# Normalizing tiles on GpSimd: mean and power applied directly, or through an offset from VectorE

## The chip, the cores and the metric

The kernel runs on one core of one Trainium2 chip. The core has five engines with a queue each: TensorE (PE; its weight loads are listed apart as PEld), VectorE (DVE), ScalarE (ACT), GpSimd (POOL) and SyncE (SP, which here issues transfers). Each works through its own instructions in order and waits on semaphores for the others. The metric is the device time of one execution in microseconds; lower is better.

## The reference, cut to what matters

A transformer block on x of shape (2, 1024, 256) with a context of (2, 154, 192), in float32, 16 heads of 64:

```python
h = _layernorm(x, ln1_g, ln1_b)
x = _attention(h, h, sa_wq, sa_wk, sa_wv, sa_wo, sa_bo) + x
h = _layernorm(x, ln2_g, ln2_b)
x = _attention(h, cond_emb, ca_wq, ca_wk, ca_wv, ca_wo, ca_bo) + x
h = _layernorm(x, ln3_g, ln3_b)
p = h @ ff_w1 + ff_b1
a, gate = (p[..., :D_FF], p[..., D_FF:])
h = a * jax.nn.gelu(gate, approximate=False) @ ff_w2 + ff_b2
return h + x
...
def _layernorm(x, g, b, eps=1e-05):
    mu = jnp.mean(x, axis=-1, keepdims=True)
    var = jnp.var(x, axis=-1, keepdims=True)
    return (x - mu) * jax.lax.rsqrt(var + eps) * g + b
```

## The kernel before, in words

All of x stays on the chip, in tiles of 128 rows by 256 columns, eight tiles for each of the two batches. The kernel has one long program, written out in order by hand: nothing reorders it. It runs in three parts. First comes self-attention (16 units of one batch and two heads, each in eight steps, loop `for p in range(SA)`), then cross-attention (16 units in three steps, loop `for c in range(CA)`), then the feed-forward (64 steps, loop `for k in range(2 * FU)`). The parts overlap: work for a later part is put on lists (`work`, `side`, `outs`, `later`, `slow`) and taken from them a piece at a time between the steps of the part that is running.

A normalization (`norm_pieces`) is cut into pieces. `stats` takes mean and variance of one tile on DVE (lines 242 and 243) into the tile `mv`. `deviation` works on a pair of tiles: it adds epsilon (line 248) and raises the result to the power −0.5 on POOL (line 252), which gives `rstd`. `normalize`, also on a pair, forms `off` = −mean · rstd on DVE (line 258, 128 x 2 elements) and then, for each of the two tiles, computes x · rstd + off. `turn` transposes the result on PE (line 286, four transposes per pair, the second of which already reads the second tile), and `store` inside it applies gain and shift (lines 297 and 301). `mv`, `var`, `rstd` and `off` come from a pool with four buffers for each name.

Which engine applies x · rstd + off depends on `narrow(kind, b)`. It is true for both batches of the first normalization and for batch 0 of the second; there ACT does it (line 276), or, in the very first normalization, ACT for one tile and POOL for the other. It is false for batch 1 of the second normalization (in the cross-attention loop) and for both batches of the third (batch 0 late in the cross-attention loop, batch 1 in the feed-forward loop); there POOL does both tiles (line 273). That makes 3 normalizations of 4 pairs each, 12 pairs and 24 POOL instructions.

`norm_beside` spreads a normalization over steps: in one step a pair gets its stats, in the next its deviation, then its normalize, then its turn. Within one step the pieces are issued as turn, (stats, put on `slow`), deviation of a later pair, normalize; so on POOL the power of the next pair stands just ahead of the normalize of this one, and on DVE the offset stands ahead of the next pair's stats.

Of the names in the trace: L901 scales the probabilities of cross-attention on POOL, after the reciprocal L898 on DVE; L650 does it in self-attention. L1074 is a matrix product of the feed-forward (`pa`, `pb`, `pc`); L1103, L1105, L1119, L1122 and L1131 are DVE's sums over those products, L1117, L1123 and L1099 are ACT's activations and copies, L1124 and L1133 POOL's products of the two halves. L500 is the output projection of an attention, L953 probabilities by values, L873 the scores of cross-attention.

Of the kernel before, what the change touches and what calls it, by code (L numbers as in the profile page):

```python
# [8 lines left out]
F32 = mybir.dt.float32  # L9
AF = mybir.ActivationFunctionType  # L10
ALU = mybir.AluOpType
AX = mybir.AxisListType

P = 128
# [4 lines left out]
def tile_transformer_block(ctx: ExitStack, tc: tile.TileContext, a: dict, out: bass.AP):  # L19
    nc = tc.nc  # L20
# [41 lines left out]
    small = ctx.enter_context(tc.tile_pool(name="small", bufs=4))  # L62
# [105 lines left out]
    for n in names[2:]:  # L168
        own = rows[row_of[n] - n_cols:row_of[n] - n_cols + n_of[n], :]
# [53 lines left out]
    def norm_pieces(kind, b, first=False):  # L223

        ln = {"sa": "ln1", "ca": "ln2", "ff": "ln3"}[kind]
        g0, b0 = row_of[ln + "_g"], row_of[ln + "_b"]  # L230
        st = {}
        nh = NC if kind == "ff" else NH
        order = tile_order(kind)

        def stats(t):
            if t == 0:
                st["hT"] = hT[kind, b] = p2.tile(
                    [P, nh, NC * S // nh], F32, tag="hT", name=f"hT_{ln}_{b}")
            if t % 2 == 0:
                st["mv", t] = small.tile([P, 2, 2], F32, tag="mv", name=f"mv_{ln}_{b}_{t}")  # L240
            s6 = small.tile([P, 6], F32, tag="st", name=f"st_{ln}_{b}_{t}")
            nc.vector.bn_stats(s6, xt[b, order[t] // GT][:, order[t] % GT, :])
            nc.vector.bn_aggr(st["mv", t // 2 * 2][:, t % 2, :], s6)

        def deviation(t):
            mv = st["mv", t]
            var = small.tile([P, 2], F32, tag="var", name=f"var_{ln}_{b}_{t}")
            (nc.vector if first else nc.gpsimd).tensor_scalar(
                var, mv[:, :, 1], EPS, 1.0, op0=ALU.add, op1=ALU.mult
            )  # L250
            rstd = small.tile([P, 2], F32, tag="rstd", name=f"rstd_{ln}_{b}_{t}")
            nc.gpsimd.tensor_tensor(rstd, var, power, ALU.pow)
            st["rstd", t] = rstd

        def normalize(t):
            rstd = st["rstd", t]
            off = small.tile([P, 2], F32, tag="off", name=f"off_{ln}_{b}_{t}")
            nc.vector.scalar_tensor_tensor(
                off, st["mv", t][:, :, 0], -1.0, rstd, op0=ALU.mult, op1=ALU.mult
            )  # L260
            if narrow(kind, b) and not first:
                xn = st["hT"][:, :, t * P // 2:(t + 2) * P // 2].rearrange(
                    "p c (i d) -> p c i d", i=2)
                st["xn", t] = [xn[:, c].rearrange("p i d -> p (i d)") for c in range(nh)]
            else:
                xn = pp_.tile([P, nh, 2, D // nh], F32, tag="P", name=f"xn_{ln}_{b}_{t}")
                flat = xn.rearrange("p c i d -> p (c i d)")
                st["xn", t] = [flat[:, i * P:(i + 1) * P] for i in range(2 * D // P)]
            for i in range(2):
                xs = xt[b, order[t + i] // GT][:, order[t + i] % GT, :]  # L270
                xs, own = xs.rearrange("p (c d) -> p c d", c=nh), xn[:, :, i, :]
                if not narrow(kind, b) or first and i == 1:
                    nc.gpsimd.tensor_scalar(
                        own, xs, rstd[:, i:i + 1], off[:, i:i + 1], op0=ALU.mult, op1=ALU.add)
                else:
                    nc.scalar.activation(
                        own, xs, AF.Identity, bias=off[:, i:i + 1], scale=rstd[:, i:i + 1])

        def turn(t):

            n = 2 if first else 1
            bank = mm_tile if first and t == 2 else spare["bank"]
            ph = [bank(f"ph_{ln}_{b}_{t}_{i}") for i in range(n)]
            for i in range(2 * D // P):

                nc.tensor.transpose(  # L286
                    ph[i * n * P // (2 * D)][:, i % (2 * D // P // n) * P:][:, :P],
                    st["xn", t][i], ident)

            def store():  # L290
                k = NC * 2 * P // nh
                for c in range(nh):
                    own = st["hT"][:, c, t // 2 * k:(t // 2 + 1) * k]
                    turned = ph[c * n // nh][:, c % (nh // n) * k:][:, :k]
                    gain, shift = cols[:, g0 + c:g0 + c + 1], cols[:, b0 + c:b0 + c + 1]
                    if spare["turned"] or first and c < nh // 2:
                        nc.vector.tensor_scalar(
                            own, turned, gain, shift, op0=ALU.mult, op1=ALU.add
                        )
                    else:  # L300
                        nc.scalar.activation(own, turned, AF.Identity, bias=shift, scale=gain)

            return store

        return (
            [lambda t=t: stats(t) for t in range(NT)],
            *([lambda t=t, f=f: f(t) for t in range(0, NT, 2)] for f in (deviation, normalize, turn)),
        )

    def tile_order(kind):  # L310

        if kind == "ff":
            return list(range(NT))
        return [t for i in range(NT // 2) for t in (i, NT // 2 + i)]

    def narrow(kind, b):

        return kind == "sa" or kind == "ca" and b < B - 1
# [947 lines left out]
    with tc.manual_schedule():  # L1266
# [11 lines left out]
        own = [ps_s.tile([P, 2, HB], F32, tag="s", name=f"first_{r}") for r in range(2)]  # L1278
# [47 lines left out]
        for p in range(SA):  # L1326
# [28 lines left out]
            if hg == LAG:  # L1355
                f = (ui - NPAIR // 2 - 1) * EC
# [184 lines left out]
```

## Time and profile before

| | us |
|---|---|
| median of 3 runs | 1070.75 (1070.31 to 1073.51) |
| the profiled execution | 1067.09 |
| its span in the trace | 1065.1 |

The profile lists, for each engine, the time in which an instruction was running. Rows of groups give line, engine, operation, output <- inputs, shape, count, then total busy time and mean nanoseconds of one, then the idle time of the engine just before and whom it waited for. Rows of the timeline give start, duration, engine, line and operation, with idle time before it in brackets. Ends of PE's matrix products are modelled, so idle time of PE is seen only where a product starts late.

### The profile page before, as it was taken

What the parts mean: (1) busy time and instruction counts of PE and PEld (TensorE: products, weight loads), DVE (VectorE), ACT (ScalarE), POOL (GpSimd) and SP (SyncE); (2) the same over time, 40 slices, a digit from 0 to 9 for tenths busy, and PEclk for the clock granted to TensorE, in tenths of its full rate; (3) what the DMA queues carried; (4) which work ended last, traced back from release to release, by engine and by line L of the source; (5) the groups of instructions that cost most, each with busy time, mean ns of one, the idle gap of its engine ahead of it and who ended that gap; (6) DMA issues with size and microseconds to landing.
All of it is one profiled execution on the core that took longest, in us unless ns stands there. A gap on an engine that the chain in (4) does not pass through costs nothing.

```text
span 1065.1 us, 48669 instructions
## 1 busy us (share of the span) xinstructions
PE 1055.6 (99%) x20228; PEld 707.7 (66%) x20228; DVE 882.5 (83%) x1321; ACT 647.3 (61%) x2096; POOL 778.4 (73%) x1652
## 2 busy tenths in 40 slices
PE   8999999999999999999999999999999999999998
PEld 6556656656555555667655655566866668788998
DVE  5789999998989989999999899979877877654555
ACT  5766767677666666666776676666666554343231
POOL 2677777778777777777777777777767875499984
PEclk9999999999999999999999999999999999999999
DMA  3131122121021121111102101126776545000000
GB/s 102 36 75 54 29 68 54 25 63 41 22 58 28 34 51 34 39 34 34 45 14 54 44 14 38 33 57 161 175 172 165 123 98 125 5 11 11 21 10 30
DMA packets 86046, 60.95 MB, mean 57 GB/s; under 512 B 32123, under 2 KB 74563, under 8 KB 85827
## 3 DMA queue, kind: packets, MB, share of 16 engines
q1 hardware_dynamic: 84450, 57.07, 22.1%
q8 instruction: 159, 2.61, 1.0%
q10 hardware_dynamic: 1376, 0.79, 0.3%
q14 instruction: 61, 0.49, 0.2%
HBM read 27.91 MB, written 2.10 MB: 28 GB/s over the span
## 4 chain that ended last, share of the span: by engine, by line
PE 90%; DVE 3%; POOL 2%; DMA 2%; SPq 1%; issue 1%; ACT 1%; DVEq 0%; POOLq 0%; ACTq 0%
PE po L578 19%; PE s L526 19%; PE py_ca L500 5%; PE py_sa L500 5%; PE pk_sa L369 5%; PE pq_sa L369 5%; PE pq_ca L369 4%; PE pv_sa L405 4%; PE poc L953 4%; PE pb L1074 4%; PE pq L1219 4%; PE sc L873 3%; PE pa L1074 2%; PE pc L1074 2%; PE pf L1249 1%; PE ph_ln L286 1%
## 5 line engine op out<-in xcount | busy, mean ns | idle before, releaser
L650 POOL TENSOR_SCALAR p<-p,rd,ee 128x512 f32<-128x512 f32 x512 | 392.6, 772 | 88.6 <-DVE rd L640 86.6
L537 ACT ACTIVATE p<-s,st 128x512 f32<-128x512 f32 x512 | 345.3, 687 | 174.1 <-DVE st L712 170.6
L712 DVE TENSOR_REDUCE st<-s 128x2 f32<-128x1024 f32 x256 | 308.7, 1207 | 57.7 <-issue 17.5
L675 DVE STREAM_TRANSPOSE pT<-p 128x1024 f32<-128x1024 f32 x256 | 302.5, 1219 | 1.6 <-POOL p L650 1.4
L526 PE MATMUL s<-k_sa,q_sa 64*32 64x512 f32 x4096 | 255.8, 591 | 0.8 <-DVE k_sa L390 0.6
L578 PE MATMUL po<-pT,held_v 64*32 64x256 f32 x8192 | 238.9, 376 | 0.0
L578 PEld LDWEIGHTS po<-pT,held_v 64*32 64x32 f32 x8192 | 178.2, 106 | 69.8 <-issue 26.5
L526 PEld LDWEIGHTS s<-k_sa,q_sa 64*32 64x32 f32 x4096 | 87.4, 106 | 93.1 <-issue 46.8
L890 ACT ACTIVATE p<-sc,neg 128x154 f32<-128x154 f32 x256 | 96.4, 406 | 73.5 <-DVE rden L898 70.6
L901 POOL TENSOR_SCALAR p<-p,rden 128x154 f32<-128x154 f32 x256 | 97.3, 401 | 47.3 <-DVE rden L898 47.0
L537 ACT ACTIVATION_READ_ACCUMULATOR p<-s,st 128x1 f32 x512 | 103.7, 203 | 0.0
L555 POOL TENSOR_TENSOR dd<-st 128x8 f32<-128x8 f32 x128 | 25.8, 202 | 69.0 <-DMA st<-st 65.1
L500 PE MATMUL py_ca<-ca_wo,o_ca 128*128 128x256 f32 x256 | 60.2, 383 | 0.0
L500 PE MATMUL py_sa<-sa_wo,o_sa 128*128 128x256 f32 x256 | 59.5, 386 | 0.0
L500 PEld LDWEIGHTS py_sa<-sa_wo,o_sa 128*128 128x128 f32 x256 | 47.3, 190 | 18.0 <-issue 5.9
L369 PE MATMUL pq_ca<-hT_ln,ca_wq 64*64 64x512 f32 (+1 forms) x576 | 58.5, 589 | 0.3 <-DMA ca_wq<-in_L_xattn_ca_wq_dram 0.3
L879 DVE TENSOR_REDUCE neg<-sc 128x6 f32<-128x924 f32 (+1 forms) x48 | 47.8, 995 | 12.1 <-PE sc L873 12.1
L369 PE MATMUL pq_sa<-hT_ln,sa_wq 64*32 64x512 f32 (+1 forms) x976 | 57.3, 586 | 0.0
L890 ACT ACTIVATION_READ_ACCUMULATOR p<-sc,neg 128x1 f32 x256 | 56.7, 221 | 0.0
L369 PE MATMUL pk_sa<-hT_ln,sa_wk 64*32 64x512 f32 x960 | 56.5, 590 | 0.1
L917 DVE STREAM_TRANSPOSE pT_ca<-p 128x480 f32<-128x480 f32 (+1 forms) x96 | 52.9, 586 | 0.9 <-POOL p L901 0.8
L500 PEld LDWEIGHTS py_ca<-ca_wo,o_ca 128*128 128x128 f32 x256 | 47.4, 190 | 8.2 <-issue 1.9
(158 smaller groups left out, 1479.5 us busy)
## 6 DMA issues: line engine op xcount, KB each, us to landing
wf<-pT_ca SPq DMA_DIRECT2D x128, 128.0 KB, 2.4
st<-st SPq DMA_DIRECT2D x512, 1.0 KB, 1.8
held_v<-held_v SPq DMA_DIRECT2D x32, 256.0 KB, 3.8
sa_wq<-in_L_xattn_sa_wq_dram SPq DMA_DIRECT2D x32, 128.0 KB, 2.9
sa_wk<-in_L_xattn_sa_wk_dram SPq DMA_DIRECT2D x32, 128.0 KB, 3.3
sa_wv<-in_L_xattn_sa_wv_dram SPq DMA_DIRECT2D x16, 256.0 KB, 4.3
ca_wq<-in_L_xattn_ca_wq_dram SPq DMA_DIRECT2D x32, 128.0 KB, 3.7
wf<-in_L_xattn_ff_w_dram SPq DMA_DIRECT2D x12, 256.0 KB, 3.1
```

Of the source, the lines that this page charges most:

```text
L369: nc.tensor.matmul(pq[r][f:f + m, at:at + n], lhsT=wt[own, c, f:f + m], rhs=h[own, c, t0:t0 + n], start=(c == 0), stop=(c == NH - 1), tile ...
L500: nc.tensor.matmul(py[:, e * D:(e + 1) * D], lhsT=o[:, i, (t + e) * P:(t + e + 1) * P], rhs=wo[kind][:, g * HP + i, :], start=(i == 0), st ...
L526: nc.tensor.matmul(sc[a4 * KB:(a4 + 1) * KB, j, :], lhsT=q[r, c:c + KB], rhs=k[r, h * HB:(h + 1) * HB], start=True, stop=True, tile_positi ...
L537: nc.scalar.activation(pr[:, j, :], sc[:, j, :], AF.Exp, bias=st[:, 0, 0, i, j:j + 1], accum_out=st[:, 0, 1, i, j:j + 1],)
L578: nc.tensor.matmul(po[a2][d:d + KB, :QH // 2], lhsT=v[e][r, t, d:d + KB], rhs=pT[r, d // DH * NK + n, :], start=(t == 0 and e == 0), stop= ...
L650: nc.gpsimd.tensor_scalar(pr[:, j, :], pr[:, j, :], own["rd"][:, c:c + 1], own["ee"][:, 0, c:c + 1], op0=ALU.mult, op1=ALU.mult,)
L675: nc.vector.transpose(halves[h][:, :, c:c + KB], slots[p]["p"][i].rearrange("p j (n k) -> p (j n) k", k=KB))
L712: nc.vector.tensor_reduce(st[:, 0, 0, i, :], sc[i], AX.X, ALU.max, negate=True)
L890: nc.scalar.activation(pr_[:, j, i, :T], sc[:, j, i * T:(i + 1) * T], AF.Exp, bias=neg[:, j, i:i + 1], accum_out=den[:, j, i:i + 1],)
L901: nc.gpsimd.tensor_scalar(pr_[:, j, i, :T], pr_[:, j, i, :T], rden[:, j, i:i + 1], 1.0, op0=ALU.mult, op1=ALU.mult,)
L917: nc.vector.transpose(pTc["ring"][:, ui % 3, :, j, t0 * KB:(t0 + nt) * KB].rearrange("p n (i q) -> p i n q", q=KB), pr_[:, j, :nt, :].rear ...
L1074: nc.tensor.matmul(into[:, :BT], lhsT=lhs, rhs=wh[pair][i], start=first, stop=True, skip_group_check=True)
```

## The change

In the three normalizations for which `narrow` is false, `normalize` no longer forms `off`. POOL's instruction subtracts the mean and multiplies by the power, taking both from the tiles `mv` and `rstd`. The other normalizations keep the offset. Lines behind the edit move down by six; in the changed kernel the new POOL instruction is on line 275, the offset on line 260.

```diff
         def normalize(t):
             rstd = st["rstd", t]
-            off = small.tile([P, 2], F32, tag="off", name=f"off_{ln}_{b}_{t}")
-            nc.vector.scalar_tensor_tensor(
-                off, st["mv", t][:, :, 0], -1.0, rstd, op0=ALU.mult, op1=ALU.mult
-            )
+            direct = not narrow(kind, b)
+            if not direct:
+                off = small.tile([P, 2], F32, tag="off", name=f"off_{ln}_{b}_{t}")
+                nc.vector.scalar_tensor_tensor(
+                    off, st["mv", t][:, :, 0], -1.0, rstd, op0=ALU.mult, op1=ALU.mult
+                )
...
-                if not narrow(kind, b) or first and i == 1:
+                if direct:
+                    nc.gpsimd.tensor_scalar(
+                        own, xs, st["mv", t][:, i, 0:1], rstd[:, i:i + 1],
+                        op0=ALU.subtract, op1=ALU.mult)
+                elif first and i == 1:
                     nc.gpsimd.tensor_scalar(
                         own, xs, rstd[:, i:i + 1], off[:, i:i + 1], op0=ALU.mult, op1=ALU.add)
```

## The prediction

> **What bounds the kernel now.** I read first the page: its busy line and the chain that ended last.
> ```profile
> span 1065.1 us, 48669 instructions
> PE 1055.6 (99%) x20228; PEld 707.7 (66%) x20228; DVE 882.5 (83%) x1321; ACT 647.3 (61%) x2096; POOL 778.4 (73%) x1652
> PE 90%; DVE 3%; POOL 2%; DMA 2%; SPq 1%; issue 1%; ACT 1%; DVEq 0%; POOLq 0%; ACTq 0%
> ```
> TensorE (PE) sets the time. Work taken from VectorE (DVE) or GpSimd (POOL) counts only where PE stands still for it. All 12 calls that the change touches lie between 727 and 950 us, so next I read the windows and, for that stretch, whom PE waited for.
> ```profile
> 727.00:950.00 223.00, 220.95 (x2513) 163.54 (x2503) 171.75 (x393) 121.00 (x520) 158.00 (x377) 1.00 0.49 115
> ```
> The columns are the stretch, its length, and busy time and instructions of PE, weight load, DVE, ACT and POOL, then the granted clock. PE stands still for 223.00 − 220.95 = 2.05 us there; the clock is full.
> ```profile
> PE pb L1074 <- DVE own L1103: 0.7, 1, 0.7
> PE ph_ln L286 <- POOL xn_ln L273: 0.6, 3, 0.2
> PE sc L873 <- ACT p L890: 0.5, 1, 0.5
> ```
> These are all the named waits of PE in the stretch (total, times, longest). The first may have an offset in its past, the second is for the changed instructions themselves, the third comes before the first offset.
>
> **The change, part by part.** Groups of the stretch from 727 to 950 us, then POOL's other two-operation groups from the whole span:
> ```profile
> L273 POOL TENSOR_SCALAR xn_ln<-x,rstd_ln,off_ln 128x256 f32<-128x256 f32 x24 | 13.1, 554 | 0.0
> L258 DVE SCALAR_TENSOR_TENSOR off_ln<-mv_ln,rstd_ln 128x2 f32<-128x2 f32 x12 | 3.5, 294 | 0.0
> ```
> ```profile
> L650 POOL TENSOR_SCALAR p<-p,rd,ee 128x512 f32<-128x512 f32 x512 | 392.6, 772 | 88.6 <-DVE rd L640 86.6 <-DMA st<-st 1.5
> L901 POOL TENSOR_SCALAR p<-p,rden 128x154 f32<-128x154 f32 x256 | 97.3, 401 | 47.3 <-DVE rden L898 47.0
> L556 POOL TENSOR_SCALAR dd<-dd 128x8 f32<-128x8 f32 x128 | 32.0, 250 | 11.8
> L248 POOL TENSOR_SCALAR var_ln<-mv_ln 128x2 f32<-128x2 f32 x20 | 3.9, 193 | 1.5
> ```
> *Removed:* 12 offsets on DVE, 3.5 us together at 294 ns. *Changed:* 24 POOL instructions keep their shape, count and place, and do subtract then multiply in place of multiply then add. *Wait removed:* POOL's wait for the offset; the last column, 0.0 us before L273, says that it costs nothing today. The orders of PE, ACT and SP are the same in both programs, no DMA moves, and DVE's order differs by the 12 offsets alone. *Wait added:* the last normalize of the feed-forward of batch 1 waits on POOL's own semaphore, for a power that POOL ended before the 938.30 row below, 3.8 us before that normalize begins at 942.09; nothing stands behind it. The mean's tile is now read until POOL has normalized. It has four buffers and one is taken per pair, so it comes round again one whole normalization later: nothing.
>
> *The price of subtract-multiply.* No row has this pair. Multiply-multiply costs (772 − 401) / (512 − 154) = 1.04 ns per element and 241 ns ahead of it; 256 elements by that line are 507 ns, and multiply-add takes 554. That is the low end. For the high end I take the small rows as another line, from add-multiply on 2 elements (193 ns) to minimum-multiply on 8 (250 ns): 9.5 ns per element if the unusual pair runs in a slow loop, and 193 + 254 × 9.5 = 2606 ns. But 250 ns is also just what the multiply-multiply line gives for 8 elements (241 + 8), without any slow loop. I take 554 ns, the nearest row: same shape, same two pointer operands, same two steps with one of them additive.
>
> By the Trainium skill (GPSIMD Engine Reference, section 3.1) a body of one or two operations per element is bound by the port, whatever they are; then the pair costs the same and this term is 0. Its section 7 speaks against the change: a dependent fp32 chain that is not unrolled takes 4 cycles per step; two steps at its 1.2 GHz are an estimate of 256 × 8 / 1.2 = 1.7 us per instruction, and the sum would be that of the first rival. The 1.04 ns per element of multiply-multiply shows an unrolled loop for that pair; no row shows it for this one.
>
> *Where POOL's price meets PE.* The timeline, each normalize (x2: both tiles) with the transposes that read it:
> ```profile
> 737.70 1.09 POOL L273 TENSOR_SCALAR xn_ln<-x,rstd_ln,off_ln 128x256 f32<-128x256 f32 x2
> 740.19 0.66 PE L286 MATMUL ph_ln<-ident,xn_ln 128*128 128x128 f32 x4
> 744.77 1.09 POOL L273 TENSOR_SCALAR xn_ln<-x,rstd_ln,off_ln 128x256 f32<-128x256 f32 x2
> 745.97 0.66 PE L286 MATMUL ph_ln<-ident,xn_ln 128*128 128x128 f32 x4
> ...
> 842.47 2.28 POOL L901 TENSOR_SCALAR p<-p,rden 128x154 f32<-128x154 f32 x6 [1.18 <-DVE rden L898]
> 845.88 1.09 POOL L273 TENSOR_SCALAR xn_ln<-x,rstd_ln,off_ln 128x256 f32<-128x256 f32 x2
> 847.02 0.55 PE L286 MATMUL ph_ln<-ident,xn_ln 128*128 128x128 f32 x3 [0.21 <-POOL xn_ln L273]
> 853.44 1.09 POOL L273 TENSOR_SCALAR xn_ln<-x,rstd_ln,off_ln 128x256 f32<-128x256 f32 x2
> 860.10 0.66 PE L286 MATMUL ph_ln<-ident,xn_ln 128*128 128x128 f32 x4
> ...
> 930.68 1.10 POOL L273 TENSOR_SCALAR xn_ln<-x,rstd_ln,off_ln 128x256 f32<-128x256 f32 x2
> 931.71 0.68 PE L286 MATMUL ph_ln<-ident,xn_ln 128*128 128x128 f32 x4
> 934.71 1.10 POOL L273 TENSOR_SCALAR xn_ln<-x,rstd_ln,off_ln 128x256 f32<-128x256 f32 x2
> 935.86 0.55 PE L286 MATMUL ph_ln<-ident,xn_ln 128*128 128x128 f32 x3 [0.21 <-POOL xn_ln L273]
> 936.25 0.60 PE L1074 MATMUL pa<-hT_ln,wf 128*128 128x256 f32 x2
> 938.30 1.10 POOL L273 TENSOR_SCALAR xn_ln<-x,rstd_ln,off_ln 128x256 f32<-128x256 f32 x2
> 941.00 0.60 PE L286 MATMUL ph_ln<-ident,xn_ln 128*128 128x128 f32 x4
> 942.09 1.10 POOL L273 TENSOR_SCALAR xn_ln<-x,rstd_ln,off_ln 128x256 f32<-128x256 f32 x2
> 946.18 0.60 PE L286 MATMUL ph_ln<-ident,xn_ln 128*128 128x128 f32 x4
> ```
> Slack between POOL's end and PE's start: 1.40 us (737.70 + 1.09 to 740.19), 0.11, 0 (847.02), 5.57 (860.10), 0 (931.71), 0 (935.86), 1.60 (941.00), 2.99 (946.18). The four pairs not shown have more than 5.57. So three places pay every nanosecond, one nearly so.
>
> *What DVE gives back.* Eight of the offsets stand in the cross-attention part and run under PE, and the only wait for POOL there that ends on PE (847.02) descends from 842.47, which is ahead of that step's offset: 0. In the feed-forward there is one place, and the timeline shows it:
> ```profile
> 928.15 0.73 POOL L1133 TENSOR_TENSOR held_v<-own 128x256 f32<-128x256 f32 x1
> 928.22 0.68 DVE L258 SCALAR_TENSOR_TENSOR off_ln<-mv_ln,rstd_ln 128x2 f32<-128x2 f32 x1
> 930.27 0.41 DVE L1103 TENSOR_TENSOR own<-pb,own 128x256 f32<-128x256 f32 x1
> 930.74 0.70 PE L1074 MATMUL pb<-hT_ln,wf 128*128 128x256 f32 x2 [0.74 <-DVE own L1103]
> 931.74 0.73 POOL L1133 TENSOR_TENSOR held_v<-own 128x256 f32<-128x256 f32 x1
> 932.22 0.60 PE L1074 MATMUL pa<-hT_ln,wf 128*128 128x256 f32 x2
> 932.95 0.73 POOL L1124 TENSOR_TENSOR kT<-own 128x256 f32<-128x256 f32 x1 [0.47 <-ACT own L1123]
> 935.84 0.68 DVE L258 SCALAR_TENSOR_TENSOR off_ln<-mv_ln,rstd_ln 128x2 f32<-128x2 f32 x1
> 937.31 0.48 DVE L1131 SCALAR_TENSOR_TENSOR own<-pb,cols,own 128x256 f32<-128x256 f32 x1 [0.79 <-PE pb L1074]
> ```
> The offset at 928.22 takes 0.68 us and DVE then runs on to L1103, for which PE waits 0.74. Without it PE starts at 930.74 − 0.68 = 930.06 and comes to the transposes 0.68 earlier, at 931.03. But they need both tiles, and POOL ends the second at 931.78 as before. After the wait at 935.86 the next product starts at 936.25, 0.44 after POOL's end at 935.81; so here it starts at 931.78 + 0.44 = 932.22, where it starts today. The gain is lost to POOL at once. What is left: the products in front ran earlier, so ACT's result for POOL at 932.95 is there by 0.47 us sooner (POOL's idle time; it can't be more), the normalize at 934.71 ends at 935.34 in place of 935.81, and the product of 936.25 starts 0.47 earlier. The offset at 935.84 is followed by 0.79 us of idle DVE: nothing. Gain in all: 0.47 us; bounds 0 and the 2.05 us of all idle PE time in the stretch.
>
> The 0.68 us fits the Trainium skill (SBUF — State Buffer, "Who interferes with whom"): a DVE instruction with two SBUF inputs contends with a POOL instruction that reads SBUF, and the first one holds the port. The trace agrees (both 0.68 us offsets stand beside an L1133), and by that rule alone the removal could give 2 × 0.68 us; the rows above say that POOL and idle DVE take most of it.
>
> **Sum.** The profiled execution's own time is 1067.09 us around a span of 1065.1; the median of the runs is 1070.75, 3.66 more. 1067.09 − 0.47 = 1066.6, and with the 3.66 the forecast is **1070.3 us**. Runs of this kernel spread from 1070.31 to 1073.51, 0.3%, so under 3.2 us I call it no change.
>
> **Rivals.**
> *Subtract-multiply is dear on POOL (slower).* Place: the transposes of L286; price: 2e per pair, e above 554 ns, less the slacks. For: no row has the pair, and the two small rows allow it; POOL is also the last to arrive three times. Against: minimum-multiply lies on the multiply-multiply line. It decides from 4 × 2e − 0.11 − 0.47 = 3.2, e = 0.47, about 1.02 us per instruction. At the 2606 ns end 2e = 4.10: 2.70 + 3.99 + 3 × 4.10 + 2.50 + 1.11 = 22.6, so 1070.75 + 22.6 = 1093; halfway (1.58 us, 2e = 2.05): 0.65 + 1.94 + 6.15 + 0.45 = 9.2, so with the 0.47 off, 1079.5.
>
> *DVE's relief reaches PE in full (faster).* All 3.5 us of offsets come off the end: 1067.2. For: PE's ends are modelled, so idle time may be hidden in busy rows, and DVE stays 77% busy in the stretch (171.75 of 223). Against: PE's shown idle time is 2.05 us, of which 0.5 (the wait for ACT) is before the first offset. With that bound, 1068.7, which is within 0.3%.
>
> *The change does not relieve DVE.* DVE's next two-input instruction meets POOL's L1133 in the offset's place and takes its 0.68 us: 1070.8. For: both dear offsets met it. Against: batch statistics follow them, with one input.
>
> **How the numbers follow.** No measurable change as worked out 0.58, no relief 0.10, relief in full 0.12, dear subtract 0.20. Dear subtract is over 0.3% in about 0.16 of the whole; relief passes 0.3% only by hidden idle time or by the spread of runs, together 0.10. So faster 0.10, same 0.74, slower 0.16. The range starts at full relief, 1067.2, and takes in the nearer part of the dear case up to 1076 (e about 0.72 us: 2e = 1.45 gives 4 × 1.45 + 0.05 − 0.11 − 0.47 = 5.3), leaving some 0.13 above and 0.05 below.
>
> **What would show it.** The new L275 group: 24 instructions at 540 to 570 ns and no idle time before them says that the pair costs the same; 1 us or more is the rival. PE's wait of 0.7 us on L1103 gone, and a wait on the normalize of about 0.6 us in its place near 931, shows the trade with POOL; the normalize some 0.5 us earlier near 934 shows what remains. DVE's busy time between 727 and 950 should fall by about 3.5 us and PE's hardly move. PE standing still less than 0.5 us there would show full relief; a change above 3.2 us with the group at 554 ns would show the reasoning wrong.

## The result and the profile after

| | before | changed |
|---|---|---|
| median of 6 runs, us | 1070.59 (1069.32 to 1073.51) | 1076.97 (1074.86 to 1079.7) |
| ratio, 95% interval | 1 | 1.0055 [1.0037, 1.0072] |
| the profiled execution, us | 1067.09 | 1075.6 |
| its span, us | 1065.1 | 1073.8 |

The change makes the kernel slower by 0.55%, some 5.9 us (the two medians lie 6.4 us apart). The forecast was no change at 1070.3 us, and the time lies above the range's end of 1076. It is the first rival that came: subtract-multiply is dear on GpSimd (POOL in the rows). The page of the changed kernel, busy line and chain:

```profile
span 1073.8 us, 48653 instructions
PE 1057.0 (98%) x20228; PEld 706.2 (66%) x20228; DVE 880.7 (82%) x1309; ACT 646.6 (60%) x2096; POOL 791.0 (74%) x1652
PE 87%; POOL 4%; DVE 3%; DMA 2%; SPq 2%; ACT 1%; issue 1%; POOLq 0%; ACTq 0%; DVEq 0%
```

PE's busy time is almost what it was, while the span is 8.7 us longer: PE stands still more. POOL's share of the chain has gone from 2% to 4%. The groups between 727 and 960 us, and whom PE waited for there (total, times, longest):

```profile
L275 POOL TENSOR_SCALAR xn_ln<-x,mv_ln,rstd_ln 128x256 f32<-128x256 f32 x24 | 29.1, 1217 | 0.0
L292 PE MATMUL ph_ln<-ident,xn_ln 128*128 128x128 f32 x48 | 8.4, 287 | 6.6 <-POOL xn_ln L275 6.5
```
```profile
PE ph_ln L292 <- POOL xn_ln L275: 6.5, 6, 2.4
PE sc L879 <- ACT p L896: 0.5, 1, 0.5
```

One instruction costs 1217 ns in place of 554, and PE waits 6.5 us for it in place of 0.6. The wait on L1103 (0.7 us before) is gone from the list, as was foreseen. The timeline shows where PE waits:

```profile
740.67 2.44 POOL L275 TENSOR_SCALAR xn_ln<-x,mv_ln,rstd_ln 128x256 f32<-128x256 f32 x2
743.18 0.66 PE L292 MATMUL ph_ln<-ident,xn_ln 128*128 128x128 f32 x4
748.91 2.42 POOL L275 TENSOR_SCALAR xn_ln<-x,mv_ln,rstd_ln 128x256 f32<-128x256 f32 x2
751.38 0.66 PE L292 MATMUL ph_ln<-ident,xn_ln 128*128 128x128 f32 x4 [2.38 <-POOL xn_ln L275]
...
852.35 0.33 PE L292 MATMUL ph_ln<-ident,xn_ln 128*128 128x128 f32 x1 [0.83 <-POOL xn_ln L275]
853.56 0.55 PE L292 MATMUL ph_ln<-ident,xn_ln 128*128 128x128 f32 x3 [0.88 <-POOL xn_ln L275]
...
911.20 0.60 PE L292 MATMUL ph_ln<-ident,xn_ln 128*128 128x128 f32 x4
...
939.69 0.55 PE L292 MATMUL ph_ln<-ident,xn_ln 128*128 128x128 f32 x3 [0.88 <-POOL xn_ln L275]
940.07 0.60 PE L1080 MATMUL pa<-hT_ln,wf 128*128 128x256 f32 x2
...
944.54 0.55 PE L292 MATMUL ph_ln<-ident,xn_ln 128*128 128x128 f32 x3 [0.87 <-POOL xn_ln L275]
944.92 0.60 PE L1080 MATMUL pa<-hT_ln,wf 128*128 128x256 f32 x2
...
954.86 0.60 PE L292 MATMUL ph_ln<-ident,xn_ln 128*128 128x128 f32 x4
```

PE waits at the same four places that have no slack, or next to none, in the prediction's list. Where the four transposes of a pair are shown as one and three, the second had to wait for the second tile. To compare executions I use one measure from here on, **the stretch**: from the start of the first transposes of these normalizations to the start of the last. It is 946.18 − 740.19 = 205.99 us before and 954.86 − 743.18 = 211.68 after, 5.69 more. That is 0.53% of the time, nearly all of the 0.55%. Of the 8.7 us between the two spans, the first transposes' 743.18 − 740.19 = 2.99 us lie ahead of any changed wait of PE; that place moves between 740.19 and 743.18 in all the kernels of this study, whose code up to there is nearly the same, so I count it as a difference between executions and not as the change's.

Where the stretch grew, piece by piece between these starts:

| piece | before | after | difference |
|---|---|---|---|
| first to second transposes (cross-attention) | 745.97 − 740.19 = 5.78 | 8.20 | +2.42 |
| to the last three transposes of the first pair of batch 0, for the feed-forward | 847.02 − 745.97 = 101.05 | 102.18 | +1.13 |
| to that normalization's last | 904.67 − 847.02 = 57.65 | 57.64 | 0 |
| to the product behind the first pair of batch 1 | 932.22 − 904.67 = 27.55 | 28.87 | +1.32 |
| to the product behind the second pair | 936.25 − 932.22 = 4.03 | 4.85 | +0.82 |
| to the last transposes | 946.18 − 936.25 = 9.93 | 9.94 | 0 |

### The profile page after: what moved, and what is told of

Read it like the earlier page. It is cut to its first block, busy times and chain, and to the rows that moved or that the text cites. A ratio compares the mean times of both kernels' runs of the same rounds, so it can differ in the third digit from the quotient of the medians.

```text
span 1073.8 us, 48653 instructions
## 1 busy us (share of the span) xinstructions
PE 1057.0 (98%) x20228; PEld 706.2 (66%) x20228; DVE 880.7 (82%) x1309; ACT 646.6 (60%) x2096; POOL 791.0 (74%) x1652
## 4 chain that ended last, share of the span: by engine, by line
PE 87%; POOL 4%; DVE 3%; DMA 2%; SPq 2%; ACT 1%; issue 1%; POOLq 0%; ACTq 0%; DVEq 0%
PE po L584 19%; PE s L532 18%; PE py_ca L506 5%; PE py_sa L506 5%; PE pk_sa L375 4%; PE pq_ca L375 4%; PE pv_sa L411 4%; PE pq_sa L375 4%; PE poc L959 4%; PE pq L1225 3%; PE pb L1080 3%; PE sc L879 3%; PE pa L1080 2%; PE pc L1080 2%; SPq L553 2%; DMA st<-st 2%
## 5 line engine op out<-in xcount | busy, mean ns | idle before, releaser
L532 PE MATMUL s<-k_sa,q_sa 64*32 64x512 f32 x4096 | 260.1, 591 | 0.8 <-DVE k_sa L396 0.6
L584 PE MATMUL po<-pT,held_v 64*32 64x256 f32 x8192 | 241.6, 376 | 0.4 <-DMA held_v<-held_v 0.4
L532 PEld LDWEIGHTS s<-k_sa,q_sa 64*32 64x32 f32 x4096 | 91.5, 106 | 90.6 <-issue 45.2
L506 PE MATMUL py_ca<-ca_wo,o_ca 128*128 128x256 f32 x256 | 60.2, 383 | 0.0
L506 PE MATMUL py_sa<-sa_wo,o_sa 128*128 128x256 f32 x256 | 59.5, 386 | 0.0
L506 PEld LDWEIGHTS py_sa<-sa_wo,o_sa 128*128 128x128 f32 x256 | 47.3, 190 | 17.9 <-ACT k_sa L398 4.2
L411 PE MATMUL pv_sa<-sa_wv,hT_ln 64*32 64x256 f32 x1792 | 53.5, 376 | 0.0
```

The lines of the kernel that those rows point to most:

```text
L411: nc.tensor.matmul(pv[r][f:f + KB, e * VC:(e + 1) * VC], lhsT=h[half, c, t0:t0 + KB], rhs=wt[half, c, :], start=(c == 0), stop=(c == NH - ...
L506: nc.tensor.matmul(py[:, e * D:(e + 1) * D], lhsT=o[:, i, (t + e) * P:(t + e + 1) * P], rhs=wo[kind][:, g * HP + i, :], start=(i == 0), st ...
L532: nc.tensor.matmul(sc[a4 * KB:(a4 + 1) * KB, j, :], lhsT=q[r, c:c + KB], rhs=k[r, h * HB:(h + 1) * HB], start=True, stop=True, tile_positi ...
L584: nc.tensor.matmul(po[a2][d:d + KB, :QH // 2], lhsT=v[e][r, t, d:d + KB], rhs=pT[r, d // DH * NK + n, :], start=(t == 0 and e == 0), stop= ...
```

## The experiments

Three questions: what does each pair of operations cost; does the price reach the end through lateness at a few places, or through GpSimd's load; and what is the removed offset worth. Each ratio below is to runs of the kernel before that were made alongside (medians 1068.38 us for e1 to e4, 1068.15 for e5 to e8).

**e1_pairs: what a pair of operations costs.** The kernel before, with this behind its last work:

```diff
+        src = xt[0, 0][:, 0, :]
+        s0, s1 = cols[:, 0:1], cols[:, 1:2]
...
+        half = probe[:, :2 * P]
+        for _ in range(3):
+            ts(half, src, s0, s1, op0=ALU.mult, op1=ALU.mult)
+            ts(half, src, s0, s1, op0=ALU.mult, op1=ALU.add)
...
```

> The kernel before, with 45 more GpSimd instructions behind its last work (each of 15 forms three times, into a scratch tile), to read the price of each pair of operations on 128x256 with pointer operands, and of two pairs on 8 and 64 elements. Theory A (the pair with the subtraction or addition in front is dear): multiply-multiply 505 to 560 ns, multiply-add 554 ns, multiply-subtract 554 ns, add-multiply and subtract-multiply 1217 ns. Theory B (subtraction itself is dear): subtract-multiply and multiply-subtract 1217 ns, add-multiply 554 ns. Theory C (every pair but a few favoured ones goes through a slow loop): add-add and minimum-multiply 1217 ns as well. Price per element of subtract-multiply between 64 and 256 elements, if it is a slower loop: (1217 - 241) / 256 = 3.8 ns; if it is a fixed charge for the instruction, 1.0 to 1.2 ns with some 650 ns more ahead of it. Time: later by the new tail, 45 instructions at 0.4 to 1.2 us = 20 to 50 us.

GpSimd's groups of the tail, by line. The lines stand in the order of the program, and the pairs are: 1514 multiply-multiply, 1515 multiply-add, 1516 add-multiply, 1517 subtract-multiply, 1518 multiply-subtract, 1519 add-add, 1520 minimum-multiply; 1521 a lone subtract, 1522 a lone multiply; 1523 and 1525 multiply-add on 8 and 64 elements, 1524 and 1526 subtract-multiply on the same; 1527 subtract-multiply and 1528 multiply-add with two constants in place of pointers.

```profile
L1519 POOL TENSOR_SCALAR probe<-x,cols 128x256 f32<-128x256 f32 x3 | 3.7, 1234 | 0.3
L1518 POOL TENSOR_SCALAR probe<-x,cols 128x256 f32<-128x256 f32 x3 | 3.7, 1233 | 0.3
L1517 POOL TENSOR_SCALAR probe<-x,cols 128x256 f32<-128x256 f32 x3 | 3.7, 1226 | 0.3
L1520 POOL TENSOR_SCALAR probe<-x,cols 128x256 f32<-128x256 f32 x3 | 3.7, 1225 | 0.3
L1527 POOL TENSOR_SCALAR probe<-x 128x256 f32<-128x256 f32 x3 | 3.2, 1068 | 0.3
L1521 POOL TENSOR_SCALAR probe<-x,cols 128x256 f32<-128x256 f32 x3 | 2.8, 927 | 0.3
L1522 POOL TENSOR_SCALAR probe<-x,cols 128x256 f32<-128x256 f32 x3 | 2.8, 925 | 0.3
L1526 POOL TENSOR_SCALAR probe<-x,cols 128x64 f32<-128x64 f32 x3 | 1.7, 578 | 0.3
L1515 POOL TENSOR_SCALAR probe<-x,cols 128x256 f32<-128x256 f32 x3 | 1.7, 555 | 0.3
L1514 POOL TENSOR_SCALAR probe<-x,cols 128x256 f32<-128x256 f32 x3 | 1.7, 554 | 0.2
L1516 POOL TENSOR_SCALAR probe<-x,cols 128x256 f32<-128x256 f32 x3 | 1.7, 554 | 0.3
L1524 POOL TENSOR_SCALAR probe<-x,cols 128x8 f32<-128x8 f32 x3 | 1.2, 409 | 0.3
L1528 POOL TENSOR_SCALAR probe<-x 128x256 f32<-128x256 f32 x3 | 1.2, 405 | 0.3
L1525 POOL TENSOR_SCALAR probe<-x,cols 128x64 f32<-128x64 f32 x3 | 1.2, 393 | 0.3
L1523 POOL TENSOR_SCALAR probe<-x,cols 128x8 f32<-128x8 f32 x3 | 1.0, 347 | 0.3
```

The one run took 1097.97 us, 29.6 more than before, within what was expected. Theory C holds: of the seven pairs tried three are cheap (multiply-multiply, multiply-add, add-multiply, 554 to 555 ns) and four cost 1225 to 1234, with the subtraction first or last or without any. A is refuted by the cheap add-multiply, B by the dear add-add and minimum-multiply. It is in the main a price per element: from 64 to 256 elements multiply-add rises by (555 − 393) / 192 = 0.84 ns an element and subtract-multiply by (1226 − 578) / 192 = 3.4, near the 3.8 that a slower loop was expected to show. What makes one pair cheap and another dear inside GpSimd, these runs do not show.

**e2_muladd: the change without the dear pair.**

```diff
                 if direct:
                     nc.gpsimd.tensor_scalar(
-                        own, xs, st["mv", t][:, i, 0:1], rstd[:, i:i + 1],
-                        op0=ALU.subtract, op1=ALU.mult)
+                        own, xs, rstd[:, i:i + 1], st["mv", t][:, i, 0:1],
+                        op0=ALU.mult, op1=ALU.add)
```

> The changed kernel, with GpSimd's instruction put back to multiply-add: x times the power plus the mean, so the output leaves out that the mean is subtracted and scaled. The offset on VectorE and the wait for it stay away. Theory (the price of subtract-multiply is all of it): GpSimd's group falls from 1217 to 554 ns, the stretch between the first and the last transposes of the three normalizations (205.99 us before, 211.68 us after the change) is 205.5, 0.5 us under before, and the time is 0.9995 of before. Rival (what was taken from VectorE, or the order of waits, costs the time): the stretch stays near 211.7 and the time near 1.0055.

The ratio is 0.9994 [0.9986, 1.0003]; GpSimd's group and PE's wait for it between 727 and 960 us:

```profile
L275 POOL TENSOR_SCALAR xn_ln<-x,rstd_ln,mv_ln 128x256 f32<-128x256 f32 x24 | 13.0, 551 | 0.0
```
```profile
PE ph_ln L292 <- POOL xn_ln L275: 0.6, 3, 0.2
```

The stretch, from 741.79 to 946.99, is 205.20: all of the loss is gone, and 0.79 us more. This kernel has no offset either, and reads the mean's tile and the power as the changed one does. So nothing that was taken from VectorE, and no order of waits, costs the time; the pair of operations does.

**e3_tight and e4_loose: does every dear instruction count?** The pairs are shared out by the slack that the profile of before shows; e4 has `and not late` in the last line, and the other pairs keep the form of before:

```diff
-            direct = not narrow(kind, b)
+            late = (kind, b, t) in (("ca", 1, 2), ("ff", 0, 0), ("ff", 1, 0), ("ff", 1, 2))
+            direct = not narrow(kind, b) and late
```

> Subtract-multiply without offset only for the 4 pairs of tiles for which TensorE arrives within 0.11 us of GpSimd's end (the second of cross-attention's batch 1, the first of the feed-forward's batch 0, the first and second of its batch 1); the other 8 pairs as before. Theory (each nanosecond counts where TensorE is there already): stretch 205.99 + 1.22 + 1.33 + 1.33 + 0.86 = 210.7, time 1.0044 of before. Rival (the load on GpSimd counts, wherever it falls): 8 of 24 instructions, a third of the 5.7 us: stretch 207.9, time 1.0018.

> The counterpart: subtract-multiply without offset only for the 8 pairs with 1.4 us of slack or more, the 4 late ones as before. Theory: 1.33 us a pair stays under the slack, but GpSimd's delay at the first pair is carried to the second (1.14 us in the changed kernel, less 0.11 of slack): stretch 205.99 + 1.0 = 207.0, time 1.0010 of before. Slack alone without carrying: 206.0, 1.0000. Rival (load counts): 16 of 24 instructions: stretch 209.8, time 1.0036.

PE's waits, first in e3_tight, then in e4_loose (there L276 is the dear form, L280 the cheap one):

```profile
PE ph_ln L293 <- POOL xn_ln L276: 5.4, 6, 1.2
```
```profile
PE ph_ln L293 <- POOL xn_ln L280: 1.6, 4, 1.0
PE pb L1081 <- DVE own L1110: 0.8, 1, 0.8
```

The four tight pairs, a third of the instructions: ratio 1.0046 [1.0034, 1.0059], stretch 951.78 − 741.09 = 210.69, which is 4.70 more than before and what was expected. The eight loose ones, two thirds: 1.0013 [1.0004, 1.0022], stretch 948.46 − 741.25 = 207.21, 1.22 more. Together that is 5.92, close to the 5.69 of the whole change. Load on GpSimd would have given the loose ones twice the loss of the tight. And most of what the loose ones do cost is PE's wait of 1.0 us for a *cheap* normalize: the dear pair ahead of it has made it late, and the second transposes start 748.12 − 741.25 = 6.87 us after the first, against 5.78 before, 1.09 more.

**e5_first: the dear pair, but issued earlier.** GpSimd's normalize stands ahead of the next pair's variance and power:

```diff
-        for fns, first in ((turn, 3), (stats, 0), (deviation, 1), (normalize, 2)):
+        pieces = ((turn, 3), (stats, 0), (deviation, 1), (normalize, 2))
+        if not narrow(kind, b):
+            pieces = pieces[:2] + pieces[:1:-1]
+        for fns, first in pieces:
```

> The changed kernel, but in the three normalizations GpSimd's normalize of a pair is issued ahead of the next pair's variance and power (0.19 + 0.71 us and their gaps, 0.99 us) instead of behind them. Theory (the price counts as lateness of GpSimd at the transposes): the normalize ends 0.99 us earlier against TensorE, so of 1.33 us extra a late pair costs 0.34 in place of 1.33; the second pair, with what is carried to it, 2.4 + 0.11 less 1.10 of slack, 1.3. Stretch 205.99 + 1.3 + 3 x 0.34 - 0.47 = 207.8 against 211.68 in the changed kernel, time 1.0017 of before. Rival (GpSimd's amount of work counts): nothing is taken away, 211.7 and 1.0055.

Ratio 1.0034 [1.0022, 1.0046], stretch 951.26 − 741.96 = 209.30: 2.38 of the 5.69 us are saved, where 3.9 were expected. GpSimd in the feed-forward, with TensorE's transposes:

```profile
933.59 2.43 POOL L275 TENSOR_SCALAR xn_ln<-x,mv_ln,rstd_ln 128x256 f32<-128x256 f32 x2
936.11 0.19 POOL L248 TENSOR_SCALAR var_ln<-mv_ln 128x2 f32<-128x2 f32 x1
936.38 0.71 POOL L252 TENSOR_TENSOR rstd_ln<-var_ln,power 128x2 f32<-128x2 f32 x1
937.06 0.73 POOL L1142 TENSOR_TENSOR held_v<-own 128x256 f32<-128x256 f32 x1
937.75 0.73 POOL L1133 TENSOR_TENSOR kT<-own 128x256 f32<-128x256 f32 x1
938.45 2.44 POOL L275 TENSOR_SCALAR xn_ln<-x,mv_ln,rstd_ln 128x256 f32<-128x256 f32 x2
```
```profile
936.08 0.55 PE L292 MATMUL ph_ln<-ident,xn_ln 128*128 128x128 f32 x3 [0.75 <-POOL xn_ln L275]
940.94 0.55 PE L292 MATMUL ph_ln<-ident,xn_ln 128*128 128x128 f32 x3 [0.87 <-POOL xn_ln L275]
```

The first of these two places costs 936.46 − 908.64 = 27.82 us against 27.55 before, 0.27 where 0.34 was expected. The second costs as much as in the changed kernel (941.32 − 936.46 = 4.86 between the products behind the transposes, against 4.03 before): GpSimd runs without a break from one normalize to the next, 938.45 − 933.59 = 4.86 us of its own work, so an earlier place in the order does not help here. Another 0.6 us came in the cross-attention step after the first of batch 0, where VectorE now waits 1.69 us for GpSimd's probabilities (0.17 before); that was not followed further. So both are at work: lateness at the first tight place of a run, GpSimd's own throughput at a tight place straight after one.

**e6_neg and e7_first_neg: versions that compute the whole block.** ScalarE negates the mean, GpSimd uses add-multiply; e7 has e5's order as well.

```diff
+            if direct:
+                neg = small.tile([P, 2], F32, tag="off", name=f"neg_{ln}_{b}_{t}")
+                nc.scalar.activation(neg, st["mv", t][:, :, 0], AF.Copy, scale=-1.0)
...
-                        own, xs, st["mv", t][:, i, 0:1], rstd[:, i:i + 1],
-                        op0=ALU.subtract, op1=ALU.mult)
+                        own, xs, neg[:, i:i + 1], rstd[:, i:i + 1],
+                        op0=ALU.add, op1=ALU.mult)
```

> A kernel that computes the whole block: ScalarE negates the mean (128x2) and GpSimd adds it and multiplies by the power, without VectorE's offset. Theory (add-multiply is one of the three cheap pairs, 554 ns): stretch as with multiply-add alone, 205.2, and time 0.9994 of before. Rival (ScalarE's small instruction stands behind its exponentials and GpSimd now waits for it): GpSimd has idle time ahead of the normalize, and the stretch is over 206.

> Both: ScalarE's negated mean with add-multiply, and the normalize ahead of the next pair's power. Theory: TensorE waits for the normalize nowhere, and what VectorE gives back near 931 us reaches TensorE; 205.99 - 0.38 - 0.74 - 0.21 = 204.7, time 0.999 of before. Rival (what GpSimd does later comes late instead): 205.2 or more.

GpSimd's groups (e6, then e7), and then TensorE's waits in e7:

```profile
L278 POOL TENSOR_SCALAR xn_ln<-x,neg_ln,rstd_ln 128x256 f32<-128x256 f32 x24 | 13.1, 552 | 0.8 <-ACT neg_ln L260 0.8
```
```profile
L278 POOL TENSOR_SCALAR xn_ln<-x,neg_ln,rstd_ln 128x256 f32<-128x256 f32 x24 | 13.1, 555 | 2.1 <-ACT neg_ln L260 2.0 <-POOL p L913 0.2
```
```profile
PE sc L885 <- ACT p L902: 0.5, 1, 0.5
PE poc L965 <- ACT q_ca L396: 0.2, 1, 0.2
```

e6: 0.9996 [0.9988, 1.0005], stretch 946.48 − 741.28 = 205.20, just as e2; GpSimd does wait for ScalarE, 0.8 us in all, but where there is slack (ahead of the normalizes at 764.39 and 877.45). e7: 0.9984 [0.9975, 0.9992], stretch 945.93 − 741.84 = 204.09 where 204.7 was expected. PE waits for no normalize any more. This version is faster than both kernels, than the one before by 0.16%.

**e8_keep_off: the changed kernel with the offset still formed.** VectorE's instruction stays for all pairs; nobody reads it for these 12.

```diff
-            if not direct:
-                off = small.tile([P, 2], F32, tag="off", name=f"off_{ln}_{b}_{t}")
+            off = small.tile([P, 2], F32, tag="off", name=f"off_{ln}_{b}_{t}")
...
```

> The changed kernel with VectorE's offset still formed for all 12 pairs, though for these nobody reads it. Theory: what the removed offset gives back is 0.47 us at the pair after the first of the feed-forward's batch 1, so the stretch is 211.68 + 0.47 = 212.2. Rival (VectorE's relief is worth nothing): 211.7.

The stretch of this one run, 954.07 − 740.57 = 213.50, is above both figures. But 1.67 us of it lie in one output projection between the second and third transposes: eight matmuls of L505 from 749.28 take 3.56 us, where those of L506 take 1.89 in the changed kernel. The clock granted to TensorE in these 3.56 us was 0.52, and 1.00 there in the changed kernel, so these 1.67 us are the clock's and not the offset's; why it fell is not known. Without the 1.67 us the stretch is 211.8, near the rival's 211.7. At the place in question the trace is plain:

```profile
938.89 0.55 PE L291 MATMUL ph_ln<-ident,xn_ln 128*128 128x128 f32 x3 [0.88 <-POOL xn_ln L274]
939.27 0.60 PE L1079 MATMUL pa<-hT_ln,wf 128*128 128x256 f32 x2
...
943.75 0.55 PE L291 MATMUL ph_ln<-ident,xn_ln 128*128 128x128 f32 x3 [0.88 <-POOL xn_ln L274]
944.13 0.60 PE L1079 MATMUL pa<-hT_ln,wf 128*128 128x256 f32 x2
```

944.13 − 939.27 = 4.86 us, the 4.85 of the changed kernel. And PE's waits show what the offset does at the pair before:

```profile
PE ph_ln L291 <- POOL xn_ln L274: 5.8, 5, 2.4
PE pb L1079 <- DVE own L1108: 0.8, 1, 0.8
```

With the offset PE waits 0.8 us for VectorE, as it did before the change (0.7), and 5.8 us for the normalize; without it, not at all for VectorE and 6.5 us for the normalize. The removed offset only changes whom PE waits for. With the dear pair it gives nothing at the place where it was expected; the theory's 0.47 is refuted here.

## Why the prediction was wrong

- **What bounds the kernel, and where the change can act:** right. PE's busy time stayed, its idle time made the difference, in the stretch named and at the four places named.
- **The price of subtract-multiply: this step failed.** It was taken as 554 ns, "the nearest row", and is 1217. The argument against a dear pair was that minimum-multiply on 8 elements (250 ns) lies on the multiply-multiply line. That line, 1.04 ns an element and 241 ns ahead, was drawn through L650 with two pointers and L901 with one pointer and one constant, and so was no line: at e1's 0.84 ns an element the charge ahead of the elements is 772 − 512 × 0.84 = 342 ns for L650 and 401 − 154 × 0.84 = 272 for L901. With two constants, as in L556, the cheap pairs go from L248's 193 ns at 2 elements (add-multiply) to 405 at 256 (multiply-add in e1), 0.83 ns each. From L556's 250 ns at 8 to the 1068 of subtract-multiply at 256 it is 3.3 each, nearly the 3.4 of e1's dear pair with pointers; and e1 shows that minimum-multiply is itself a dear pair (1225 ns). So the row that spoke against the rival was a row of the rival. The prediction did name this reading, as its upper end of 2606 ns, which was twice too high because it drew its line through one cheap and one dear row.
- **The rule of the Trainium skill** (GPSIMD Engine Reference, section 3.1) that one or two operations per element cost the same does not hold here: 554 against 1226 ns for two operations, and 925 for one. The estimate from the Trainium skill's section 7 on the same page, 1.7 us, spoke against the change; it was more than the 1.22 measured, but had the sign. That a dependent chain is what makes the pair dear, no run shows.
- **How a price becomes time: a term was missing.** The mechanism, lateness at the transposes, was right. With e = 0.66 the prediction's own sum gives 1.22 + 3 × 1.33 − 0.47 = 4.7 us, which with its 1070.75 is 1075.5, still inside the range; measured are 5.69. At the second pair 1.22 was expected and 2.42 came, since the first pair's delay was counted as hidden in its 1.40 us of slack. It was hidden from PE, but GpSimd had next to no idle time to make it up (busy 7.99 of the 8.24 us): from the first normalize to the second it took 748.91 − 740.67 = 8.24 us, against 744.77 − 737.70 = 7.07 before, and was 1.17 us later at the next one. e4_loose shows that delay by itself (+1.09 at the second transposes). At the other three places 3 × 1.33 − 0.47 = 3.5 was expected and 1.13 + 1.32 + 0.82 = 3.27 came. The 0.82 looks like 1.33 − 0.47, but by luck: e8 has it with the offset in place (4.86 against 4.03). What is saved there is idle time that GpSimd had before the change (0.47 us at 932.95) and that the longer normalize fills.
- **What VectorE gives back:** right for the cheap pair. The prediction said 0 at the first of batch 1 and 0.47 at the second; e6 has 933.04 − 905.51 = 27.53 against 27.55, and 936.54 − 933.04 = 3.50 against 4.03, so 0.02 and 0.53, a little over the 0.47 that was held to be the most. The rest of e6's 0.79 us is in cross-attention, 0.24, where nothing was expected; how it comes there was not followed. Beside the dear pair it is worth nothing in the feed-forward (e8).
- **The added wait and the longer life of the mean's tile:** GpSimd has no idle time ahead of L275 in the changed kernel (0.0 in its group), and VectorE none ahead of the instruction that writes the next means (L243), so both are free as forecast.
- **The chances:** 0.20 for the dear pair was too little for a price that no row showed. The range reached to about 1.27 us a piece, and so took in the price that came; but it was worked out without the delay that is carried over, and the time passed its end.

## What to carry to other kernels

An operation that no row of the trace shows is a new price even when its shape, operands and engine are known: time it by itself before arguing from a neighbour, and draw lines only through rows with the same kinds of operands. On an engine that runs almost without gaps, slack at one place is not free: of a delay of 1.33 us that hid there, 1.17 arrived at the next place. A small instruction taken off an engine that is not last gains only what the next engine in line leaves of it, here 0.79 us of 3.5 beside the cheap pair.

## What was not expected of the hardware

On GpSimd a lone multiply or subtract by a pointer (925 and 927 ns on 128x256) costs more than multiply-multiply, multiply-add or add-multiply (554 to 555). So a multiply-multiply whose second factor is 1 should be cheaper than the lone multiply; that was not run. Two pointers in place of two constants add about 150 ns to either kind: 555 against 405 for multiply-add, 1226 against 1068 for subtract-multiply.
